# Transposing the activations on VectorE in 32x32 blocks, with both batches interleaved, in a two-layer graph network

## The chip, the cores and the metric

The kernel runs on one core of one Trainium2 chip. A core has TensorE (matmuls and transposes through the array, results in PSUM), VectorE, ScalarE and GpSimd (elementwise work), and a sync engine that only issues DMA transfers here. SBUF is the on-chip memory of 128 partitions, PSUM the matmul output[...]. The metric is the device time of one execution in microseconds (us). The profiles call the engines PE, DVE, ACT and POOL; PEld is TensorE's weight load, SPq the sync engine's queue.

## The reference

64 batches of 256 tokens with 512 features, all in fp32, go through two layers, each with a layer norm, a ReLU and a residual. The first multiplies by an adjacency matrix over the tokens and then by a weight; the second is masked attention with 8 heads.

```python
# x: (64, 256, 512)   adj: (256, 256)   all weights: (512, 512)
h = jnp.maximum(_layernorm(x, axis=-1), 0.0)
x = x + jnp.einsum('bnd,do->bno', jnp.einsum('nm,bmd->bnd', adj, h), L0_weight) + L0_bias
h = jnp.maximum(_layernorm(x, axis=-1), 0.0)
q, k, v = (h @ W + b split into 8 heads of 64, for Wq, Wk, Wv)
scores = jnp.einsum('bqhd,bkhd->bhqk', q, k) / 8 + (1.0 - adj) * -1e9
out = jnp.einsum('bhqk,bkhd->bqhd', softmax(scores), v)
x = x + out.reshape(b, n, d) @ Wo + bo
```

## The kernel before

The batches are taken in 32 groups of two (`GB = 2`, `NT = 2` tiles of 128 tokens per batch, `T = 4` tiles per group, `DC = 4` chunks of 128 features). The five projections (w, q, k, v, o) each use seven products of half-size blocks in place of eight (a Strassen-like form); one product is 4 matmuls of 256 columns, and an fp32 matmul shows up as two instructions in the trace.

A program in Python lays out every engine's instructions in one fixed order. `after(delay, fn)` puts work off by so many ticks, and a `yield` of a projection is one tick. PSUM banks are handed out in the order in which they were given back:

```python
    def bank(shape, name):
        i = free_banks.pop(0)
        ...
    def give(t):
        free_banks.append(bank_of.pop(id(t))[0])
```

The features must lie on the partitions for q, k and v, so the normalised activations h1 are transposed by TensorE and copied from PSUM to `h1T`; then GpSimd forms the differences t1 to t4 for the seven products:

```python
    def queries_keys(g):
        ...
        h1T = act.tile([P, DC, GN], F32, tag="bT", name=f"h1T_{g}")
        halves = H1T[g] = Halves(f"h_{g}", [h1T[:, d, :] for d in range(DC)])
        for t in range(T):
            ps = bank([P, DC, P], f"ph_{g}_{t}")
            for d in range(DC):
                nc.tensor.transpose(ps[:, d, :], h1[:, t, d * P:(d + 1) * P], ident)
            if t % 2:
                nc.vector.tensor_copy(h1T[:, :, t * P:(t + 1) * P], ps)
            else:
                nc.scalar.copy(h1T[:, :, t * P:(t + 1) * P], ps)
            give(ps)
        for c in range(2):
            halves.sums(nc.gpsimd, c, ("t1", "t2"))
        for c in range(2):
            halves.sums(nc.gpsimd, c, ("t3", "t4"))
        yield
```

A projection. `read` and `finish` take a bank's partial result out, in the output projection by VectorE (`x <- o_a, x`); the product with `s2` adds to bank `pa` after `read(pa, 1)`:

```python
    def project(s, halves, by_token, name, read, finish, first_half_first=False):
        pa = new("a")
        product(pa, s, "a11", halves, "b11", by_token, stop=False)     # 1st product
        u1 = read(pa, 1)
        yield
        ...
        pb = new("b")
        product(pb, s, "a12", halves, "b21", by_token)                 # 2nd
        finish(pb, u1, 0, 0)
        give(pb)
        yield
        product(pa, s, "s2", halves, "t2", by_token, start=False, stop=False)   # 3rd
        u2 = read(pa, 2)
        yield
        ...  # 4th: s1 t1 into pc; 5th: s3 t3 into pa; 6th: a22 t4 into pd; 7th: s4 b22 into pc
```

`b11` to `b22` are blocks of the transposed activations themselves, t1 to t4 their differences. In q and k the activations are the moving operand of the matmul, in v the stationary one (the weight load).

The scores of a group and half of the heads: four rounds (c, b) of matmuls into two banks, two evictions by VectorE and a subtraction by GpSimd each:

```python
    def score(g, qd):
        for c in range(2):
            for b in range(GB):
                ps = [bank([P, NT * N], f"sc_{g}_{qd}_{c}{b}_{j}") for j in range(2)]
                ... # matmuls
                for j in range(2):
                    nc.vector.scalar_tensor_tensor(a[...], ps[j], SCALE, maskT_f, op0=ALU.mult, op1=ALU.add)
                    give(ps[j])
                nc.gpsimd.tensor_tensor(a, a, top_b, op=ALU.subtract)
                after(3 + 2 * c + b, exponent, a)
                after(5 + 2 * c + b, key_sum, g, qd, c, b)
```

The steady loop. `attend` is the attention product pav with the softmax denominator pden, `post` the output projection of the group before, `layer0` the first layer of the group after the next:

```python
    for g in range(NG):
        attend(g, 0)
        score(g, 1)
        tick()
        if g > 0:
            run(post(g - 1))
        if g + 2 < NG:
            load(g + 2)
            ready(g + 2, 6)
        if g + 1 < NG:
            run(queries_keys(g + 1))
        ...
        attend(g, 1)
        if g + 1 < NG:
            score(g + 1, 0)
        tick()
        if g + 1 < NG:
            run(values(g + 1))
        if g + 2 < NG:
            run(layer0(g + 2))
```

Of the kernel before, what the change touches and what calls it, by code (L numbers as in the profile page):

```python
# [8 lines left out]
F32 = mybir.dt.float32  # L9
I32 = mybir.dt.int32  # L10
AF = mybir.ActivationFunctionType
ALU = mybir.AluOpType
AX = mybir.AxisListType
P = 128
# [184 lines left out]
def kernel(  # L199
# [56 lines left out]

    clock, later = [0], []

    def after(delay, fn, *args):
        later.append((clock[0] + delay, len(later), fn, args))  # L260

    def tick():
        clock[0] += 1
        due = sorted(e[:2] for e in later if e[0] <= clock[0])
        run_now = [e for d in due for e in later if e[:2] == d]
        later[:] = [e for e in later if e[0] > clock[0]]
        for _, _, fn, args in run_now:
            fn(*args)

    X, H0, Q, K, V, OT, HO = {}, {}, {}, {}, {}, {}, {}  # L270

    def load(g):
        X[g] = xpool.tile([P, T, D], F32, tag="x", name=f"x_{g}")
        src = x[g * GB:(g + 1) * GB].rearrange("b (t p) d -> p (b t) d", p=P)
        for t in range(0, T, 1 if g == 0 else T):
            e = t + (1 if g == 0 else T)
            nc.sync.dma_start(X[g][:, t:e, :], src[:, t:e, :])

# [3 lines left out]


    load(0)
    adj_sb = tmp.tile([P, NT, N], F32, tag="u", name="adj_sb")
    nc.sync.dma_start(adj_sb, adj.rearrange("(t p) m -> p t m", p=P))
# [26 lines left out]

    adjT = const.tile([P, NT, N], F32, name="adjT")
    pa = bank([P, NT, N], "pa")
    for k in range(NT):
        for t in range(NT):
            nc.tensor.transpose(pa[:, k, t * P:(t + 1) * P], adj_sb[:, t, k * P:(k + 1) * P], ident)
    nc.vector.tensor_copy(adjT, pa)
# [7 lines left out]
    def masks():  # L327
        nc.vector.tensor_scalar(maskT, adjT, -1.0, 1.0, op0=ALU.mult, op1=ALU.add)
        nc.vector.tensor_scalar(maskT, maskT, MASKED, None, op0=ALU.mult)
        nc.vector.tensor_scalar(adj_sb, adj_sb, -1.0, 1.0, op0=ALU.mult, op1=ALU.add)  # L330
        nc.vector.tensor_scalar(adj_sb, adj_sb, MASKED, None, op0=ALU.mult)
        rowmax = small.tile([P, NT], F32, tag="rowmax", name="rowmax", bufs=1)
        nc.vector.tensor_reduce(rowmax, adj_sb, AX.X, ALU.max)
        spread = tmp.tile([P, NT, P], F32, tag="u", name="spread")
        nc.vector.tensor_copy(spread, rowmax[:, :, None].to_broadcast([P, NT, P]))
        pt = bank([P, N], "pt")
        for t in range(NT):
            nc.tensor.transpose(pt[:, t * P:(t + 1) * P], spread[:, t, :], ident)
        nc.vector.tensor_copy(top, pt)
        give(pt)  # L340
# [16 lines left out]


    def weight_sums(eng, w, name):
        def part(i, j):  # L360
            return w[:, 2 * j:2 * j + 2, i * HF:(i + 1) * HF]
        s = {n: const.tile([P, 2, HF], F32, name=f"{name}_{n}") for n in ("s1", "s2", "s4")}
        eng.tensor_tensor(s["s1"], part(1, 0), part(1, 1), op=ALU.add)
        eng.tensor_tensor(s["s2"], s["s1"], part(0, 0), op=ALU.subtract)
        eng.tensor_tensor(part(1, 0), part(0, 0), part(1, 0), op=ALU.subtract)
        eng.tensor_tensor(s["s4"], part(0, 1), s["s2"], op=ALU.subtract)
        s.update(a11=part(0, 0), a12=part(0, 1), a22=part(1, 1), s3=part(1, 0))
        return s

    class Halves:  # L370

        def __init__(self, name, chunks):
            self.chunks = chunks
            self.t = {n: act.tile([P, 2, N], F32, tag="t", name=f"{n}_{name}", bufs=8)
                      for n in ("t1", "t2", "t3", "t4")}

        def b(self, j, k, c):
            return self.chunks[2 * j + c][:, k * N:(k + 1) * N]

# [9 lines left out]
    def product(ps, s, a, halves, b, by_token, start=True, stop=True):  # L389
        for m in range(2):  # L390
            for c in range(2):
                w, y = s[a][:, c, :], halves.operand(b, c)
                lhs, rhs = (y, w) if by_token else (w, y)
                nc.tensor.matmul(ps[:, m, :], lhs[:, m * P:(m + 1) * P], rhs, start=(start and m + c == 0), stop=(c == 1),  # L394
                                 skip_group_check=True)
# [71 lines left out]

    H1, H1T = {}, {}

    def layer0(g):  # L470
# [3 lines left out]
        yT = act.tile([P, DC, GN], F32, tag="bT", name=f"yT_{g}")  # L474
        halves = Halves(f"y_{g}", [yT[:, d, :] for d in range(DC)])
        for d in (0, 2, 1, 3):
# [15 lines left out]
        st = [small.tile([P, 2, nc.vector.BN_STATS_DIM], F32, tag="st1", name=f"st1_{g}_{t}", bufs=8) for t in range(T)]  # L492
        h1 = H1[g] = act.tile([P, T, D], F32, tag="h", name=f"h1_{g}")
        done = []
# [19 lines left out]

        yield from project(W0, halves, True, f"w_{g}", read, finish)

    def queries_keys(g):

        xt, h1 = X[g], H1.pop(g)
        h1T = act.tile([P, DC, GN], F32, tag="bT", name=f"h1T_{g}")  # L520
        halves = H1T[g] = Halves(f"h_{g}", [h1T[:, d, :] for d in range(DC)])
        for t in range(T):
            ps = bank([P, DC, P], f"ph_{g}_{t}")
            for d in range(DC):
                nc.tensor.transpose(ps[:, d, :], h1[:, t, d * P:(d + 1) * P], ident)  # L525
            if t % 2:
                nc.vector.tensor_copy(h1T[:, :, t * P:(t + 1) * P], ps)  # L527
            else:
                nc.scalar.copy(h1T[:, :, t * P:(t + 1) * P], ps)
            give(ps)  # L530
        for c in range(2):
            halves.sums(nc.gpsimd, c, ("t1", "t2"))
        for c in range(2):
            halves.sums(nc.gpsimd, c, ("t3", "t4"))
        yield

        def out_bias_add(t):
            nc.gpsimd.tensor_tensor(xt[:, t, :], xt[:, t, :], bo_r, op=ALU.add)  # L538

        for s, bias, store, n in ((WQ, bq_c, Q, "q"), (WK, bk_c, K, "k")):  # L540
            store[g] = {}
# [14 lines left out]
            if n == "k":  # L556
                for t in range(T):
                    after(2 * t + 1, out_bias_add, t)
            yield from project(s, halves, False, f"{n}_{g}", read, finish)

    def values(g):
# [13 lines left out]

        yield from project(WV, halves, True, f"v_{g}", read, finish)

    def post(g):

        xt = X.pop(g)  # L580
        halves = HO.pop(g)
        done = []

        def read(ps, n):
            o = quarter(xt, *RESIDUAL[n])
            add(o, ps, o)

        def finish(ps, u, i, k):
            o = quarter(xt, i, k)
            add(o, ps, o)  # L590
            done.append(k)
            if done.count(k) == 2:
                nc.sync.dma_start(out[g * GB + k].rearrange("(t p) d -> p t d", p=P), xt[:, k * NT:(k + 1) * NT, :])

        yield from project(WO, halves, True, f"o_{g}", read, finish, first_half_first=g == NG - 1)

    A, AS = {}, {}

    def score(g, qd):


        for c in range(2):
            for b in range(GB):
# [8 lines left out]
                for j in range(2):  # L612
                    nc.vector.scalar_tensor_tensor(a[:, j * NT:(j + 1) * NT, :].rearrange("p k n -> p (k n)"),  # L613
                                                   ps[j], SCALE, maskT_f, op0=ALU.mult, op1=ALU.add)
                    give(ps[j])
                nc.gpsimd.tensor_tensor(a, a, top_b, op=ALU.subtract)  # L616
                after(3 + 2 * c + b, exponent, a)
                after(5 + 2 * c + b, key_sum, g, qd, c, b)

# [3 lines left out]
    def key_sum(g, qd, c, b):  # L623
        s = AS[c, b] = att.tile([P, 2, N], F32, tag=f"as{c}{b}", name=f"as_{g}_{qd}_{c}{b}")
        a4 = A[c, b].rearrange("p (j k) n -> p j k n", j=2)
        nc.gpsimd.tensor_tensor(s, a4[:, :, 0, :], a4[:, :, 1, :], op=ALU.add)  # L626

    def attend(g, qd):
# [21 lines left out]
        chunks = OT.setdefault(g, [])  # L650
        chunks += o
        nc.scalar.activation(den, pd, AF.Identity, accum_out=stats[:, 0, i:i + 1])  # L652
# [4 lines left out]

        def divide():
            for f in range(2):
                nc.vector.tensor_tensor(o[f], po[f], rden, op=ALU.mult)  # L660
                give(po[f])
            nc.scalar.activation(den, rden, AF.Identity, accum_out=stats[:, 1, i:i + 1])
            if qd == (0 if g == NG - 1 else 1):
                HO[g] = Halves(f"o_{g}", chunks)
                for c in range(2):
                    HO[g].sums(nc.gpsimd, c, ("t1",))
            if qd == 1:
                for which in ("t2",), ("t3", "t4"):
                    for c in range(2):
                        HO[g].sums(nc.gpsimd, c, which)  # L670

# [11 lines left out]
    for _ in range(T + 1):  # L683
        tick()
    W0 = weight_sums(nc.gpsimd, w0_sb, "w0")
    for _ in range(T + 2):
# [4 lines left out]
    run(first, 3)  # L691
    WQ = weight_sums(nc.gpsimd, wq_sb, "wq")
    run(first)
    first = queries_keys(0)
    run(first, 1)
    WK = weight_sums(nc.gpsimd, wk_sb, "wk")
    run(first, 5)
    WV = weight_sums(nc.gpsimd, wv_sb, "wv")
    out_bias()
    ready(1, 0)  # L700
    run(first)
    WO = weight_sums(nc.gpsimd, wo_sb, "wo")
    score(0, 0)
    run(values(0))
    run(layer0(1))
    for g in range(NG):
        attend(g, 0)
        score(g, 1)
        tick()
# [65 lines left out]
```

## Time and profile before

The time is 2839.26 us, the median of three runs (2838.41 to 2841.76). The profiled execution spans 2840.6 us at a granted TensorE clock of 0.997.

| group of instructions | count | busy us | mean ns of one |
|---|---|---|---|
| POOL score subtraction (L616), 128x1024 | 256 | 597.1 | 2368 |
| DVE score eviction (L613), 128x512 | 512 | 311.9 | 681 |
| DVE reciprocal (L656), 128x128 | 256 | 231.8 | 926 |
| PE first-layer product py (L480), 256 columns | 1024 | 229.3 | 382 |
| PE transposes ph (L525), 128x128 | 512 | 63.0 | 276 |
| PEld of those transposes | 512 | 58.7 | 143 |
| DVE copy h1T<-ph (L527), 128x512 | 64 | 44.0 | 690 |
| ACT copy h1T<-ph (L529), 128x512 | 64 | 37.4 | 585 |
| POOL difference t_h<-h1T (L387), 128x256 | 128 | 92.8 | 725 |

Busy time is the time in which at least one instruction of the group ran; the mean of one is longer than busy time over count where instructions overlap, as TensorE's do. From start to start, a steady product of eight matmul instructions takes 1.73 us, and the 16 transposes of a group 1.98 us. Transfers: a load of x (1 MB) lands 5.4 us after its issue, an output of 512 KB 2.8 us after, a `bv_c` transfer of 0.2 KB 2.0 us after.

Two things help in reading what follows. In a timeline a row's end is its start plus its duration, but TensorE's modelled ends overlap the next start, so for TensorE starts are compared with starts. And a share of busy time says which engine is full, not which wait ends last in a given stage.

### The profile page before, as it was taken

What the parts mean: (1) busy time and instruction counts of PE and PEld (TensorE: products, weight loads), DVE (VectorE), ACT (ScalarE), POOL (GpSimd) and SP (SyncE); (2) the same over time, 40 slices, a digit from 0 to 9 for tenths busy, and PEclk for the clock granted to TensorE, in tenths of its full rate; (3) what the DMA queues carried; (4) which work ended last, traced back from release to release, by engine and by line L of the source; (5) the groups of instructions that cost most, each with busy time, mean ns of one, the idle gap of its engine ahead of it and who ended that gap; (6) DMA issues with size and microseconds to landing.
All of it is one profiled execution on the core that took longest, in us unless ns stands there. A gap on an engine that the chain in (4) does not pass through costs nothing.

```text
span 2840.6 us, 43306 instructions
## 1 busy us (share of the span) xinstructions
PE 2799.5 (99%) x17680; PEld 2301.5 (81%) x17680; DVE 1478.2 (52%) x2703; ACT 851.7 (30%) x1441; POOL 1882.6 (66%) x1754
## 2 busy tenths in 40 slices
PE   6999999999999999999999999999999999999998
PEld 5788888888888888888888888888888888888886
DVE  3454545545555445455455554455554555545545
ACT  2332323323223233233232332332322323323221
POOL 5766666767567676676665676756766656767565
PEclk9999999999999999999999999999999999999999
DMA  4000000000000000000000000000000000000000
GB/s 130 1 1 30 31 31 30 1 30 31 31 31 21 11 30 31 30 31 1 30 31 31 30 16 16 30 31 31 30 1 30 31 31 31 10 22 30 31 16 31
DMA packets 39563, 75.97 MB, mean 27 GB/s; under 512 B 3520, under 2 KB 3776, under 8 KB 39360
## 3 DMA queue, kind: packets, MB, share of 16 engines
q1 hardware_dynamic: 39360, 73.15, 7.5%
q8 instruction: 141, 2.31, 0.3%
q14 instruction: 62, 0.51, 0.1%
HBM read 39.59 MB, written 33.55 MB: 26 GB/s over the span
## 4 chain that ended last, share of the span: by engine, by line
PE 96%; POOL 2%; DVE 1%; issue 1%; DMA 0%; ACT 0%; SPq 0%; DVEq 0%; POOLq 0%; ACTq 0%
PE sc L608 8%; PE py L480 8%; PE pav L638 8%; PE pden L644 2%; PE ph L525 2%; POOL a L616 1%; DVE x L441 0%; DVE a L613 0%; DMA adj_sb<-in_adj_dram 0%; PE q_0a L394 0%; PE o_25a L394 0%; PE o_17a L394 0%; PE o_5a L394 0%; PE o_7a L394 0%; PE o_4a L394 0%
## 5 line engine op out<-in xcount | busy, mean ns | idle before, releaser
L616 POOL TENSOR_TENSOR a<-a,top 128x1024 f32<-128x1024 f32 x256 | 597.1, 2368 | 189.0 <-DVE a L613 189.0
L53 POOL TENSOR_TENSOR rs<-rs,mhalf 128x2 f32<-128x2 f32 (+1 forms) x96 | 77.6, 809 | 553.9 <-DVE nb L52 553.9
L613 DVE SCALAR_TENSOR_TENSOR a<-sc,maskT 128x512 f32<-128x512 f32 x512 | 311.9, 681 | 230.1 <-PE sc L608 230.1
L626 POOL TENSOR_TENSOR as<-a 128x512 f32<-128x512 f32 x256 | 317.9, 1282 | 0.3 <-ACT a L621 0.3
L621 ACT ACTIVATE a<-a 128x1024 f32<-128x1024 f32 x256 | 266.7, 1054 | 136.6 <-POOL a L616 136.6
L608 PE MATMUL sc<-q,k 64*128 64x256 f32 x2048 | 250.1, 384 | 0.0
L608 PEld LDWEIGHTS sc<-q,k 64*128 64x128 f32 x2048 | 205.3, 186 | 45.5 <-PE pden L644 25.5
L480 PE MATMUL py<-adjT,h 128*128 128x256 f32 x1024 | 229.3, 382 | 6.7 <-ACT h L458 6.7
L512 ACT ACTIVATE h<-x,nb,rs 128x512 f32<-128x512 f32 x128 | 97.2, 806 | 460.6 <-POOL nb L54 460.6
L638 PE MATMUL pav<-a,v 128*32 128x256 f32 x4096 | 234.3, 381 | 0.0
L656 DVE RECIPROCAL rden<-den 128x128 f32<-128x128 f32 x256 | 231.8, 926 | 4.6 <-ACT den L652 4.6
L460 POOL TENSOR_TENSOR x<-x,b_r 128x512 f32<-128x512 f32 x128 | 162.5, 1282 | 103.2 <-ACT h L458 103.2
L480 PEld LDWEIGHTS py<-adjT,h 128*128 128x128 f32 x1024 | 196.4, 192 | 34.3 <-ACT h L458 7.4
L638 PEld LDWEIGHTS pav<-a,v 128*32 128x32 f32 x4096 | 126.5, 110 | 98.2 <-issue 21.2
L538 POOL TENSOR_TENSOR x<-x,bo_r 128x512 f32<-128x512 f32 x128 | 162.5, 1271 | 0.0
L482 ACT COPY yT<-py 128x512 f32<-128x512 f32 x128 | 75.0, 586 | 223.8 <-PE py L480 223.8
L387 POOL TENSOR_TENSOR t_h<-h1T 128x256 f32<-128x256 f32 x128 | 92.8, 725 | 72.8 <-DVE h1T L527 72.8
L458 ACT ACTIVATE h<-x,nb,rs 128x512 f32<-128x512 f32 x128 | 96.4, 806 | 11.0 <-POOL nb L54 11.0
L504 DVE BATCH_NORM_STATS2 st<-x 128x6 f32<-128x256 f32 x256 | 96.4, 419 | 4.4
L387 POOL TENSOR_TENSOR t_o<-oT,t_o 128x256 f32<-128x256 f32 x128 | 93.3, 743 | 7.8 <-DVE oT L660 7.8
L387 POOL TENSOR_TENSOR t_y<-yT,t_y 128x256 f32<-128x256 f32 x128 | 92.9, 726 | 5.8 <-ACT yT L482 0.8
L387 POOL TENSOR_TENSOR t_h<-h1T,t_h 128x256 f32<-128x256 f32 x128 | 92.8, 725 | 5.0
(2950 smaller groups left out, 5550.1 us busy)
## 6 DMA issues: line engine op xcount, KB each, us to landing
out_dram<-x SPq DMA_DIRECT2D x64, 512.0 KB, 2.8
x<-in_x_dram SPq DMA_DIRECT2D x31, 1024.0 KB, 5.4
x<-in_x_dram SPq DMA_DIRECT2D x4, 256.0 KB, 3.7
w_sb<-in_L_gnn_weight_dram SPq DMA_DIRECT2D x1, 1024.0 KB, 8.3
wq_sb<-in_L_gnn_Wq_dram SPq DMA_DIRECT2D x1, 1024.0 KB, 11.2
wk_sb<-in_L_gnn_Wk_dram SPq DMA_DIRECT2D x1, 1024.0 KB, 12.2
wv_sb<-in_L_gnn_Wv_dram SPq DMA_DIRECT2D x1, 1024.0 KB, 12.2
wo_sb<-in_L_gnn_Wo_dram SPq DMA_DIRECT2D x8, 128.0 KB, 4.6
```

The lines of the kernel that those rows point to most:

```text
L387: eng.tensor_tensor(self.t[n][:, c, :], self.operand(p, c), self.operand(q, c), op=ALU.subtract)
L460: nc.gpsimd.tensor_tensor(xt[:, t, :], xt[:, t, :], b0_r, op=ALU.add)
L480: nc.tensor.matmul(ps[:, b * N:(b + 1) * N], h[:, b * NT + k, d * P:(d + 1) * P], adjT[:, k, :], start=(k == 0), stop=(k == NT - 1))
L512: nc.scalar.activation(h1[:, k * NT + t, :], xt[:, k * NT + t, :], AF.Relu, bias=nb[:, t:t + 1], scale=rs[:, t:t + 1])
L538: nc.gpsimd.tensor_tensor(xt[:, t, :], xt[:, t, :], bo_r, op=ALU.add)
L608: nc.tensor.matmul(ps[j][:, kt * N:(kt + 1) * N], k[j * HD:(j + 1) * HD, c, kt * P:(kt + 1) * P], q[j * HD:(j + 1) * HD, c, :], start=True ...
L613: nc.vector.scalar_tensor_tensor(a[:, j * NT:(j + 1) * NT, :].rearrange("p k n -> p (k n)"), ps[j], SCALE, maskT_f, op0=ALU.mult, op1=ALU.add)
L616: nc.gpsimd.tensor_tensor(a, a, top_b, op=ALU.subtract)
L621: nc.scalar.activation(a, a, AF.Exp)
L626: nc.gpsimd.tensor_tensor(s, a4[:, :, 0, :], a4[:, :, 1, :], op=ALU.add)
L638: nc.tensor.matmul(po[f][h * 32:(h + 1) * 32, b * N:(b + 1) * N], v[:, k, h * HD + f * 32:h * HD + f * 32 + 32], A[h // 2, b][:, (h % 2) * ...
L656: nc.vector.reciprocal(rden[:, c * P:(c + 1) * P], den[:, c * P:(c + 1) * P])
```

## The change

TensorE's transposes of h1 are taken away from group 2 on. VectorE transposes h1 instead: one instruction transposes each 32x32 block of a 128x512 tile within its own block position, and writes the two batches alternately, so that an element of batch 0 is followed by that of batch 1. What remains, the move of blocks between partitions, is done by 16 transfers from SBUF to SBUF per group (one for each pair of a source and a target strip of 32 partitions) in runs of 512 bytes: 2 token tiles x 32 tokens x 2 batches x 4 bytes. So that those runs are contiguous, the tokens of a tile are permuted by blocks of 32: x is loaded and out is stored in eight transfers of 32 partitions per group, adjT is built from a permuted adjacency, and the division writes its output in permuted order (four instructions of 256 in place of two of 512). The purpose is to free TensorE of the transposes and the two engines of the copies that followed them.

With it go: h1T is read with a step of two elements; the tiles t1 to t4 have 4 buffers in place of 8, which makes room for the new tile `r`; the differences for the output projection (`out_sums`) are formed at the head of the next round in place of after the division; the key sums of the second half come four ticks later; the mask is transposed separately from adjT. Groups 0 and 1 keep TensorE's transposes, with copies that interleave.

The core of the diff (cuts marked with ...; left out are the bookkeeping of `after` and `tick`, the renaming of the weight tables and the forms of `Halves` and `product` for a stepped block):

```diff
@@ load
-        src = x[g * GB:(g + 1) * GB].rearrange("b (t p) d -> p (b t) d", p=P)
-        for t in range(0, T, 1 if g == 0 else T):
-            e = t + (1 if g == 0 else T)
-            nc.sync.dma_start(X[g][:, t:e, :], src[:, t:e, :])
+        src = x[g * GB:(g + 1) * GB]
+        for k in range(GB):
+            for i in range(NI):
+                nc.sync.dma_start(X[g][32 * i:32 * i + 32, k * NT:(k + 1) * NT, :], by_block(src, i)[:, k])
@@ adjacency
+    for i in range(NI):
+        nc.sync.dma_start(adj_r[32 * i:32 * i + 32], by_block(adj[None], i)[:, 0])
...
+    for u in range(NT):
+        nc.vector.tensor_copy(adj_p[:, u, :].rearrange("p (t i b) -> p i t b", i=NI, t=NT),
+                              adj_r[:, u, :].rearrange("p (i t b) -> p i t b", i=NI, t=NT))
...
     def masks():
-        nc.vector.tensor_scalar(maskT, adjT, -1.0, 1.0, op0=ALU.mult, op1=ALU.add)
+        pm = bank([P, NT, N], "pm")
+        for k in range(NT):
+            for t in range(NT):
+                nc.tensor.transpose(pm[:, k, t * P:(t + 1) * P], adj_sb[:, t, k * P:(k + 1) * P], ident)
+        nc.vector.tensor_scalar(maskT, pm, -1.0, 1.0, op0=ALU.mult, op1=ALU.add)
@@ Halves
-            self.t = {n: act.tile([P, 2, N], F32, tag="t", name=f"{n}_{name}", bufs=8)
+            self.t = {n: act.tile([P, 2, N], F32, tag="t", name=f"{n}_{name}", bufs=4)
@@ end of layer0
+        h1T = act.tile([P, DC, N, GB], F32, tag="bT", name=f"h1T_{g}")
+        H1T[g] = [h1T[:, d].rearrange("p n k -> p k n") for d in range(DC)]
+        if g < 2:
+            ...   # TensorE's transposes as before, copies of 128x128 that interleave
+            return
+        r = act.tile([P, DC * NI, NT, 32, GB], F32, tag="r", name=f"r_{g}")
+        def turn(k):
+            for t in range(NT):
+                nc.vector.transpose(r[:, :, t, :, k], h1[:, k * NT + t, :].rearrange("p (j b) -> p j b", b=32))
+        def turn_last():
+            turn(1)
+            blocks = r.rearrange("p (d j) t b k -> p j d (t b k)", j=NI)
+            for i in range(NI):
+                for j in range(NI):
+                    nc.sync.dma_start(h1T[32 * j:32 * j + 32, :, 64 * i:64 * i + 64, :].rearrange("p d n k -> p d (n k)"),
+                                      blocks[32 * i:32 * i + 32, j])
+        turn(0)
+        TURN[g] = turn_last
@@ queries_keys
-        ...   # the four transposes and copies shown above
@@ score: between() is turn_last of the next group
                 nc.gpsimd.tensor_tensor(a, a, top_b, op=ALU.subtract)
+                if between and c + b == 0:
+                    between()
                 after(3 + 2 * c + b, exponent, a)
-                after(5 + 2 * c + b, key_sum, g, qd, c, b)
+                after((5 if qd == 0 else 9) + 2 * c + b, key_sum, g, qd, c, b)
@@ attend, divide
             for f in range(2):
-                nc.vector.tensor_tensor(o[f], po[f], rden, op=ALU.mult)
+                for k in range(GB):
+                    ...   # dst and src of 256, dst in the permuted order
+                    nc.vector.tensor_tensor(dst, src, den_k, op=ALU.mult)
                 give(po[f])
...
-            if qd == 1:   # the differences of the output projection
-                ...
+            if g == NG - 1:
+                out_sums(g, ("t1",) if qd == 0 else ("t2", "t3", "t4"))
@@ post
-                nc.sync.dma_start(out[g * GB + k].rearrange("(t p) d -> p t d", p=P), xt[:, k * NT:(k + 1) * NT, :])
+                for i in range(NI):
+                    nc.sync.dma_start(by_block(out[g * GB:(g + 1) * GB], i)[:, k],
+                                      xt[32 * i:32 * i + 32, k * NT:(k + 1) * NT, :])
@@ the loop
         attend(g, 0)
-        score(g, 1)
+        if g > 0:
+            out_sums(g - 1)
+        score(g, 1, TURN.get(g + 1) if g > 0 else None)
```

## The prediction

> **What bounds the kernel now.** I read the page from the top: busy shares, then the chain that ended last, then one group of two batches in the order of time.
>
> ```profile
> PE 2799.5 (99%) x17680; PEld 2301.5 (81%) x17680; DVE 1478.2 (52%) x2703; ACT 851.7 (30%) x1441; POOL 1882.6 (66%) x1754
> ...
> PE 96%; POOL 2%; DVE 1%; issue 1%; DMA 0%; ACT 0%; SPq 0%; DVEq 0%; POOLq 0%; ACTq 0%
> ```
>
> TensorE is busy 99% of the span and 96% of the closing chain; the other engines are far from full. So a microsecond off TensorE's list is a microsecond off the total, unless TensorE then waits. Whether it waits is not seen in shares, so I take the timeline of group 16, TensorE and then VectorE (start, duration, engine, line, operation):
>
> ```profile
> 1417.92 3.66 PE L638 MATMUL pav<-a,v 128*32 128x256 f32 x64
> ...
> 1422.37 4.09 PE L608 MATMUL sc<-q,k 64*128 64x256 f32 x32
> 1426.39 1.99 PE L394 MATMUL o_14a<-wo_sb,oT 128*128 128x256 f32 x8
> 1428.22 1.89 PE L394 MATMUL o_14b<-wo_sb,oT 128*128 128x256 f32 x8
> 1429.95 1.98 PE L394 MATMUL o_14a<-wo_s,t_o 128*128 128x256 f32 x8
> ...
> 1438.73 1.91 PE L525 MATMUL ph<-ident,h 128*128 128x128 f32 x16
> 1440.71 1.97 PE L394 MATMUL q_16a<-h1T,wq_sb 128*128 128x256 f32 x8
> ```
>
> ```profile
> 1421.15 0.16 DVE L52 TENSOR_SCALAR nb<-mv 128x2 f32<-128x2 f32 x1
> 1423.61 4.87 DVE L613 SCALAR_TENSOR_TENSOR a<-sc,maskT 128x512 f32<-128x512 f32 x8 [2.29 <-PE sc L608]
> 1428.40 0.94 DVE L656 RECIPROCAL rden<-den 128x128 f32<-128x128 f32 x1
> 1429.26 0.62 DVE L441 TENSOR_TENSOR x<-o_14a,x 128x512 f32<-128x512 f32 x1
> ```
>
> Put the zero at 1417.92, where the attention product pav begins. TensorE runs without a break: pav and den to 4.45, scores to 8.47, seven products of the output projection of 1.73 each from start to start, the transposes (ph) from 20.81 to 22.79, then q. The transposes hold TensorE for 1.98 us per group; one period (w_16a at 1405.64 to w_17a at 1492.67) is 87.03 us.
>
> The second fence shows what the first hides. The third output product adds to the bank of the first, which VectorE must have read (x<-o_14a). That read ends at 1429.26 + 0.62 = 1429.88, and the third product starts at 1429.95: 0.07 us later. VectorE is only half busy overall, yet **from the first score eviction (5.69) to this read (11.96) it has no gap and sets TensorE's pace to within 0.07 us**. Anything put into that stretch of VectorE is paid by TensorE.
>
> [...] The interleaved h1T has a step of two fp32, 8 bytes[...]. TensorE reads no stepped operand in the rows I rest on, so no run here shows it. [...]the contiguous subtraction takes 725 ns here. [...] The trace has no such instruction; its 512-element instructions have a start-to-start step of (4.87 - 0.68)/7 = 0.60 us, which I take for a transpose of 512 elements. [...]0.2 KB lands in 2.0 us, 512 KB in 2.8.
>
> **The change part by part**, groups 2 to 31 (30 of them; 0 and 1 keep TensorE's transposes).
>
> Removed: 16 transposes, 1.98 us of TensorE; two h1T copies on VectorE (690 ns) and two on ScalarE (585 ns), all behind the seventh product.
>
> Added on VectorE: four transposes. The first two (batch 0) stand behind the last norm scale, which ends at 1421.15 + 0.16 = 3.39, and wait for the first two h rows (two at 806 ns from 2.52, ends 4.04). Ends about 5.3, before the scores want VectorE at 5.69: free. The other two stand between the first and second pair of score evictions. Their input (ScalarE's second h pair) is there at 5.93, and the first pair ends near 7.0, so they wait for nothing, but push the six later evictions, the reciprocal and x<-o_a back by 2 x 0.60 = 1.2 us. The read that ended at 11.96 ends at 13.2, the third product starts at about 13.25 in place of 12.03: **1.2 us of new wait on TensorE**. The first product is late on the way too (its bank is that of the third eviction: about 0.5), but that lies inside the 1.2. Later reads have slack: the fifth product waits for a read that ended 0.8 before it started. The division as four instructions of 256 in place of two of 512 adds some 0.3, behind this point.
>
> From the third product to the end of the projection is 1438.73 - 1429.95 = 8.78. So q can start at 13.25 + 8.78 = 22.03, where it starts at 22.79 now: **0.76 us saved per group** of the 1.98.
>
> The transport: the 16 transfers are issued from about 8.3, when the last transpose is done. At the start of the trace small transfers are issued every 0.47 us:
>
> ```profile
> 25.06 0.42 SPq L302 DMA_DIRECT2D wo_sb<-in_L_gnn_Wo_dram  x1
> 25.53 0.42 SPq L303 DMA_DIRECT2D bv_c<-in_L_gnn_bv_dram  x1
> 26.00 0.43 SPq L302 DMA_DIRECT2D wo_sb<-in_L_gnn_Wo_dram  x1
> ```
>
> 16 x 0.47 = 7.5; with 2.0 to 2.8 to land they are there at about 18.3, against 22.0 when q asks: 3.7 us in hand.
>
> GpSimd: the output projection's differences (8 x 0.69 = 5.5) move in front of the score subtractions (9.34), because the four t tiles are now shared. It is free at about 4.4, so 4.4 + 5.5 + 9.3 = 19.2; then h's t1 and t2 (4 x 0.69) are done at 22.0, and q's third product wants them at 22.0 + 3.5. Free, with 3.5 us in hand.
>
> Start: adjT needs four transfers of 32 rows, two VectorE copies and then the transposes (about +1). The mask is made from its own TensorE transposes, which stand behind the first py product, and its VectorE chain (0.68 + 0.43 + 0.42 + 0.43 + 0.69 + 0.68 = 3.3) must end before the pt transposes that stand ahead of the second py product. Now that chain runs before py and hides. Mask transposes about 0.8, chain 3.3, and the 1: +5 us once. The stepped copies of groups 0 and 1 and the four output transfers at the end: +1. At the end GpSimd sums the keys before the output differences, which may take away the two waits of 1.15 and 0.59 on pden: -1.
>
> Sum: 2839.3 - 30 x 0.76 (22.8) + 5 = **2821 us**.
>
> **The rivals.** *The wait does not come* (the transposes find a gap, or finish sooner): all 1.98 stays, 59 us, and the total is 2839 - 59 + 5 = 2785. Against it: the 0.07 us above. For it: the pacing chain is seen at the resolution of one group. *Slower transposes*: at double, 1.2 us each, the wait is 2.4 and the first pair also pushes the scores by about 0.8; a group then loses 1.2, and the total is about 2880. Nothing in the trace tells against a half rate for fp32. *The transport is late*: each microsecond beyond the 3.7 in hand costs 30 us. A transfer waits for the one eight before it, so landing in over 8 x 0.47 = 3.8 us would slow the issue as well; 512-byte runs are not in the trace at this place. *The stepped operand*: three of the seven products of q, of k and of v read h1T itself. If a stepped moving operand ran at half speed, q and k would lose 6 x 1.73 = 10.4 us per group, 311 in all, and the total would pass 3100; for v the stepped side is the weight load, which has room (190 of about 379 ns).
>
> **Range and chances.** The main estimate moves with the transpose: 0.55 to 0.75 us each gives a wait of 1.1 to 1.5, a saving of 0.9 to 0.5 per group, and 2818 to 2830. The start is good to 2 us. The range 2788 to 2852 takes in nearly all of the no-wait rival and a late transport by one microsecond. Faster by over 2% needs less than 2782.5, which even the no-wait rival just misses: 0.12. Slower by over 2% needs 2896: a stepped-operand loss, a late transport by over 2 us, or slow transposes together with something else: 0.09.
>
> **What would show it.** In the changed profile: TensorE busy about 2740 (480 transposes of 0.123 us gone); the period near 86.3; idle time of some 1.2 us per group ahead of the third output product (or split with the first), released by VectorE's x<-o read; transposes of 600 to 700 ns on VectorE; issues of h1T every 0.47 us, and no idle time of q's first product that ends with a transfer; q's and k's matmuls still 379 ns; t_h still 725 ns; w_0a some 5 us later than 26.82. If q's first product waits for a transfer, the transport was mis-sized; if TensorE is busier than before, the stepped read is not free; if the third product starts without a wait, my chain through VectorE was wrong.

## The result and the profile after

The changed kernel takes **2832.9 us** (median of 4 runs, 2831.99 to 2835.19) against 2840.12 us for the kernel before (4 runs, the earlier ones among them): ratio 0.9976, 95% interval 0.9959 to 0.9993. The change gains 7.2 us where 18 had been forecast. The two lines of the page that answer to those shown before, busy shares and closing chain:

```profile
PE 2757.9 (97%) x17204; PEld 2254.2 (80%) x17204; DVE 1531.5 (54%) x2905; ACT 821.0 (29%) x1393; POOL 1886.7 (67%) x1754
...
PE 90%; DVE 8%; issue 1%; POOL 0%; SPq 0%; DMA 0%; ACT 0%; DVEq 0%; POOLq 0%; ACTq 0%
```

TensorE has lost 476 instructions and 41.6 us, but its share fell to 97%, and VectorE, 1% of the closing chain before, holds 8% of it. TensorE now waits for VectorE. Where, the timeline of group 16 shows, TensorE first:

```profile
1413.93 3.66 PE L699 MATMUL pav<-a,v 128*32 128x256 f32 x64
...
1422.74 1.99 PE L416 MATMUL o_14a<-wo_sb,oT 128*128 128x256 f32 x8 [0.27 <-DVE a L665]
1424.58 1.89 PE L416 MATMUL o_14b<-wo_sb,oT 128*128 128x256 f32 x8
1427.23 1.97 PE L416 MATMUL o_14a<-wo_s,t_o 128*128 128x256 f32 x8 [0.77 <-DVE x L463]
...
1435.99 1.98 PE L416 MATMUL q_16a<-h1T,wq_sb 128*128 128x256 f32 x8
1437.80 1.97 PE L416 MATMUL q_16b<-h1T,wq_sb 128*128 128x256 f32 x8
1439.61 1.89 PE L416 MATMUL q_16a<-t_h,wq_s 128*128 128x256 f32 x8
```

and VectorE beside it:

```profile
1419.62 1.29 DVE L665 SCALAR_TENSOR_TENSOR a<-sc,maskT 128x512 f32<-128x512 f32 x2 [0.90 <-PE sc L660]
1420.82 1.29 DVE L563 STREAM_TRANSPOSE r<-h 128x512 f32<-128x512 f32 x2
1422.04 3.64 DVE L665 SCALAR_TENSOR_TENSOR a<-sc,maskT 128x512 f32<-128x512 f32 x6
1425.61 0.93 DVE L717 RECIPROCAL rden<-den 128x128 f32<-128x128 f32 x1
1426.46 0.62 DVE L463 TENSOR_TENSOR x<-o_14a,x 128x512 f32<-128x512 f32 x1
```

Put the zero again where pav begins, 1413.93. The pair of transposes stands between the second and the third eviction without a gap, the read of the first product ends at 13.15, the third product starts at 13.30 and q at 22.06. The waits of 0.27 and 0.77 us in brackets are the new ones, and they are all that TensorE waits for in this period of 86.70 us: it is busy for 85.66 of it.

One thing more is new, and no wait shows it. From the start of q_16b to that of the third product of q it is 1.81 us (1437.80 to 1439.61). Before it was 1.73:

```profile
1442.51 1.89 PE L394 MATMUL q_16b<-h1T,wq_sb 128*128 128x256 f32 x8
1444.24 1.91 PE L394 MATMUL q_16a<-t_h,wq_s 128*128 128x256 f32 x8
```

The trace says how long one matmul takes; the rows are those of q_16b, minimum, median and maximum in ns, first of the kernel before, then of the changed one:

```profile
L394 PE MATMUL q_16b<-h1T,wq_sb x8: 379/379/379, 1442.5 to 1444.0; 128*128 128x256 f32 x8
```

```profile
L416 PE MATMUL q_16b<-h1T,wq_sb x8: 385/388/388, 1437.8 to 1439.4; 128*128 128x256 f32 x8
```

The stage of q and k (from q_16a to the pav behind it) takes 25.17 us (1435.99 to 1461.16) where it took 24.75 (1440.71 to 1465.46). Five of the six products that read h1T itself are 0.08 to 0.09 us longer, which makes the 0.42; the sixth, q_16a, took 1.80 already before, right behind the transposes, and takes 1.81.

For everything that follows I take the period over the whole steady part, (start of v_31a - start of v_1a)/30 from each profile: **87.05 us before, 86.68 after**.

### The profile page after: what moved, and what is told of

Read it like the earlier page. It is cut to its first block, busy times and chain, and to the rows that moved or that the text cites. A ratio compares the mean times of both kernels' runs of the same rounds, so it can differ in the third digit from the quotient of the medians.

```text
span 2831.6 us, 44124 instructions
## 1 busy us (share of the span) xinstructions
PE 2757.9 (97%) x17204; PEld 2254.2 (80%) x17204; DVE 1531.5 (54%) x2905; ACT 821.0 (29%) x1393; POOL 1886.7 (67%) x1754
## 4 chain that ended last, share of the span: by engine, by line
PE 90%; DVE 8%; issue 1%; POOL 0%; SPq 0%; DMA 0%; ACT 0%; DVEq 0%; POOLq 0%; ACTq 0%
PE pav L699 8%; PE py L502 8%; PE sc L660 5%; DVE a L665 4%; PE pden L705 2%; DVE r L563 1%; DVE rden L717 1%; DVE x L463 1%; PE q_0a L416 0%; PE v_22a L416 0%; PE v_21a L416 0%; PE v_19a L416 0%; PE v_17a L416 0%; PE v_16a L416 0%; PE v_14a L416 0%
## 5 line engine op out<-in xcount | busy, mean ns | idle before, releaser
L660 PEld LDWEIGHTS sc<-q,k 64*128 64x128 f32 x2048 | 205.4, 186 | 45.1 <-PE pden L705 13.2
L409 POOL TENSOR_TENSOR t_y<-yT 128x256 f32<-128x256 f32 x128 | 93.5, 731 | 30.6 <-ACT yT L504 30.6
```

The lines of the kernel that those rows point to most:

```text
L409: eng.tensor_tensor(self.t[n][:, c, :], self.operand(p, c), self.operand(q, c), op=ALU.subtract)
L660: nc.tensor.matmul(ps[j][:, kt * N:(kt + 1) * N], k[j * HD:(j + 1) * HD, c, kt * P:(kt + 1) * P], q[j * HD:(j + 1) * HD, c, :], start=True ...
```

## The experiments

Two theories, which the expectations call S and V. **S**: the moving operand with a step of 8 bytes costs each product that reads h1T itself some 0.08 us, and this ate the missing part. **V**: the rest is VectorE's chain from the evictions to the first reads; whatever is put into it, TensorE waits for. Their rivals: the transposed layout has nothing to do with the matmuls' length (other traffic, the transfers), or the transport or GpSimd holds q up.

| kernel | median us | ratio to before (95%) | period us |
|---|---|---|---|
| changed kernel | 2832.9 | 0.9976 (0.9959 to 0.9993) | 86.68 |
| e1_before_stepped | 2855.2 | 1.0054 (1.0040 to 1.0068) | 87.53 |
| e2_apart | 2818.7 | 0.9921 (0.9908 to 0.9935) | 86.16 |
| e3_invert_late | 2816.0 | 0.9914 (0.9901 to 0.9928) | 85.95 |
| e4_turn_twice | 2867.6 | 1.0096 (1.0080 to 1.0111) | 87.87 |
| e5_mask_early | 2827.8 | 0.9949 (0.9936 to 0.9963) | 86.68 |
| e6_apart_late | 2799.5 | 0.9857 (0.9842 to 0.9872) | 85.48 |
| e7_best | 2800.1 | 0.9861 (0.9846 to 0.9876) | 85.55 |
| e9_mask_apart_late | 2791.5 | 0.9826 (0.9813 to 0.9839) | 85.53 |
| e10_turn_after_evictions | 2789.3 | 0.9819 (0.9805 to 0.9832) | 85.39 |

**e1_before_stepped**: the kernel before with nothing but the interleaved h1T.

```diff
-        h1T = act.tile([P, DC, GN], F32, ...)
+        h1T = act.tile([P, DC, N, GB], F32, ...)
-                nc.vector.tensor_copy(h1T[:, :, t * P:(t + 1) * P], ps)
+                nc.vector.tensor_copy(h1T[:, :, (t % NT) * P:(t % NT + 1) * P, t // NT], ps)
```

> The kernel before with one edit: h1T is stored with the two batches interleaved, so that q and k read a moving operand with a step of two elements; TensorE's transposes stay, nothing is carried by transfers. Theory S (a stepped moving operand costs TensorE about 0.08 us per product): q's and k's products on h1T go from 1.73 to 1.81 us from start to start, v's stay at 1.73, a period grows by about 0.42 us and the total by 13 us, to about 2853 (ratio 1.0047). Rival R (the longer products in the changed kernel come from the transfers or from the other order of work beside them, not from the step): products stay at 1.73 and the total at 2840.

```profile
L394 PE MATMUL q_16b<-h1T,wq_sb x8: 387/388/388, 1445.9 to 1447.4; 128*128 128x256 f32 x8
```

The 388 ns are here without VectorE's transposes, without transfers and without permuted tokens. The period grows by 0.48 us, the total by 15 us; in group 16 no wait is added (q_21a alone waits, 0.4 us for a copy). S holds for the step alone.

**e2_apart**: the changed kernel, the batches kept apart in `r` and h1T, so that the transfers run in 256 bytes instead of 512.

```diff
-        h1T = act.tile([P, DC, N, GB], F32, ...)
+        h1T = act.tile([P, DC, GB, N], F32, ...)
-        r = act.tile([P, DC * NI, NT, 32, GB], F32, ...)
+        r = act.tile([P, NI, DC, GB, NT, 32], F32, ...)
```

> The changed kernel with the batches apart again: VectorE writes the transposes batch by batch and the 16 transfers write runs of 256 bytes in place of 512, twice as many. Theory S: all of q's and k's products take 1.73 us, and where the transport is still in time the period falls from 86.68 to 86.27 and the total by about 12 us to 2821. If an issue grows with the number of runs (0.66 us now for 128 runs, up to 1.3 for 256), the 16 take up to 21 us, h1T lands some 10 us too late and the total rises by up to 300 us. Rival R: products stay at 1.81.

```profile
L416 PE MATMUL q_16b<-h1T,wq_sb x8: 379/379/380, 1432.5 to 1434.1; 128*128 128x256 f32 x8
```

The 379 ns are back, the period falls by 0.52 us and the total by 14 us, while the waits on VectorE stay (0.28 and 0.76). Twice as many runs of half the length did not hold the transport up: the 16 issues took 11.36 us against 10.76, and q waited for none of them. Together with e1 this closes the missing part from both sides.

**e3_invert_late**: the changed kernel, the reciprocals and the division one tick later, so that the first reciprocal stands behind x<-o_a instead of ahead of it.

```diff
-            after(1 + c, invert, c)
-        after(5, divide)
+            after(2 + c, invert, c)
+        after(6, divide)
```

> The changed kernel with the four reciprocals and the division one tick later, so that VectorE reads the first output product before the first reciprocal (0.87 us) and not after it. Theory V (the wait of the third output product is VectorE's chain of evictions, transposes, reciprocal and read): the wait of 0.77 us goes, the 0.27 ahead of the first product stays, the period falls by 0.75 to about 85.9 and the total by 23 us to about 2810 (ratio 0.989). Rival: another wait of about the same length (GpSimd's t_o, or h1T's landing, which comes 1.1 us before q asks) takes its place and the total stays near 2833.

```profile
1414.74 1.99 PE L416 MATMUL o_14a<-wo_sb,oT 128*128 128x256 f32 x8 [0.27 <-DVE a L665]
...
1418.42 1.97 PE L416 MATMUL o_14a<-wo_s,t_o 128*128 128x256 f32 x8
```

The 0.77 us ahead of the third product are gone, the period is 0.73 us shorter, and the total falls by 17 us. That is less than the 23 expected: 30 x 0.73 are 22, but in the profiles v_1a comes 2.7 us later and the end takes 0.4 us more; what is left of the difference is within the spread of the runs. Moving the reciprocals and the division by one tick, which made nothing cheaper, was worth more than the whole change.

**e4_turn_twice**: the second pair of transposes done twice.

```diff
             turn(1)
+            turn(1)
```

> The changed kernel with the second pair of transposes done twice, in the same place (the second time over the first, the result is the same). Theory V: each extra pair is paid in full, about 1.2 us per group, 30 x 1.2 = 37 us, total about 2870; the h1T transfers are issued 1.2 us later as well and q, which starts 1.2 us later, still finds them. Rival (VectorE's chain has slack of its own, and the waits seen come from elsewhere): much less than 37 us.

```profile
1443.71 1.99 PE L416 MATMUL o_14a<-wo_sb,oT 128*128 128x256 f32 x8 [1.45 <-DVE a L666]
...
1448.20 1.97 PE L416 MATMUL o_14a<-wo_s,t_o 128*128 128x256 f32 x8 [0.76 <-DVE x L463]
```

Two more transposes, 2 x 0.60 us, and TensorE pays 1.18 more ahead of the first product; the period grows by 1.19. V holds to within 0.02 us. Note the place: the first product's bank comes from the third eviction, so work ahead of that eviction is paid there, and the third product's wait stays as it was.

**e5_mask_early**: the mask moved ahead of the first layer-0 group.

```diff
+    masks()
     first = layer0(0)
-    run(first, 1)
-    masks()
-    run(first, 3)
+    run(first, 4)
```

> The changed kernel, with the whole of masks() (its four transposes and its VectorE chain) moved ahead of the first layer-0 group, so that the chain no longer stands between the first adjacency products and the transposition of them; nothing else is moved. Prediction as on record: the changed start costs 4.3 us that the end keeps, so taking it away should give about 4 us back (about 2829 us against 2833, ratio to the kernel before about 0.996). Rival, from the trace of the changed kernel: the first groups are held by GpSimd's sums, which absorbed most of the delay (v_0a is 6.1 us later than before, q_1c only 0.8 us later), so the total moves by under 1.5 us, and the first adjacency products earn a lead that is gone by v_1a.

The period is unchanged to 0.01 us and the total falls by 5.1 us (the runs of the two kernels don't overlap): the rival, which was my own reading of one pair of profiles, falls. In that pair v_1a was only 1.2 us later after the change than before it, and I took the delay for absorbed. Over all profiles but those of the runs with a step on adjT (last below), v_1a is at 164.4 and 167.9 with the start of the kernel before, at 169.1 to 172.0 in the six with the changed start (mean 170.5), at 162.8, 165.5 and 166.7 in the three with the early mask. These are one profile of each kernel, so the kernels differ a little too; but the five runs of this one kernel also lie 6.2 us apart (2823.6 to 2829.8). The scatter is as large as what I had read from a single pair. The means say 4.3 us lost by the changed start, 5.5 regained by the early mask, both uncertain by some microseconds.

Why the chain was dear: VectorE's rows in the changed kernel, then the same operations before (where the mask is made ahead of the first py product):

```profile
21.17 1.00 DVE L349 TENSOR_SCALAR maskT<-maskT 128x512 f32<-128x512 f32 x1
22.09 1.48 DVE L350 TENSOR_SCALAR adj_sb<-adj_sb 128x512 f32<-128x512 f32 x1
23.61 1.37 DVE L351 TENSOR_SCALAR adj_sb<-adj_sb 128x512 f32<-128x512 f32 x1
```

```profile
14.60 0.43 DVE L329 TENSOR_SCALAR maskT<-maskT 128x512 f32<-128x512 f32 x1
14.94 0.42 DVE L330 TENSOR_SCALAR adj_sb<-adj_sb 128x512 f32<-128x512 f32 x1
```

In the changed kernel GpSimd worked without a gap from 15.60 on (weight sums and bias sums of 1.27 us); before, this run of sums began at 15.83, behind VectorE's rows. The lengths of these rows go with that: 0.42 us ahead of the sums (GpSimd was then on an operation of 128x4), 1.00 to 1.48 beside them. The early mask of e5_mask_early splits the same chain over both cases, as GpSimd's sums begin at 16.00 there:

```profile
15.57 0.42 DVE L350 TENSOR_SCALAR adj_sb<-adj_sb 128x512 f32<-128x512 f32 x1
16.02 1.52 DVE L351 TENSOR_SCALAR adj_sb<-adj_sb 128x512 f32<-128x512 f32 x1
```

The row ahead of the sums takes 0.42 us (1.48 in the changed kernel), the one beside them 1.52. So three profiles show that the length goes with GpSimd's sums; what in the hardware makes it so was not shown.

**e6_apart_late**: e2 and e3 together.

> The changed kernel with both repairs that the earlier runs named: the batches kept apart in the transposed activations (q, k products with an unstepped moving operand) and the reciprocals and the division one tick later (no wait ahead of the third output product). If the two gains are independent, the period is 86.15 - 0.7 = about 85.4 us and the total about 2818.7 - 17 = 2800 us (ratio 0.986). Rival: the transport is the next wait. In the changed kernel GpSimd got the transposed activations 20.98 us after the zero and q started at 22.06; in this kernel q would start at about 21.2, and the four sums behind the arrival need some 0.6 us each, so part of the gain comes back as waits of the q products on GpSimd or on the transfers: then period about 85.8 and total about 2809 us.

Period 85.48 us, total 2799.5. The two gains add up: 0.52 + 0.73 = 1.25 of expected fall, 1.20 measured. In group 16 GpSimd began on h1T 21.22 us after the start of pav and q began at 21.26, so the transport now has nothing in hand; in five other groups q waits 0.3 to 0.7 us, in the longest case (q_12a) for the transfers by name.

**e7_best**: e6 with the second pair of transposes behind the first read, and two issuing queues.

```diff
-                    nc.sync.dma_start(h1T[32 * j: ...
+                    (nc.scalar if j % 2 else nc.sync).dma_start(h1T[32 * j: ...
-        score(g, 1, TURN.get(g + 1) if g > 0 else None)
+        score(g, 1)
...
+            p = post(g - 1)
+            next(p)
+            TURN[g + 1]()   # where the next group has one
+            tick()
+            run(p)
```

> The kernel of e6_apart_late with two more edits: the second pair of transposes is issued after the first output product has been read rather than ahead of the score evictions' end, and the 16 transfers are shared by two issuing queues (SyncE's and ScalarE's). Theory V: the 0.28 us ahead of the first output product goes too, and the transfers' later start (about 1 us) is more than made up by two queues (issue 16 x 0.66 = 10.6 us becomes 5.3 us), so period about 85.1 and total about 2791 us (ratio 0.983). Rival: ScalarE, which now issues eight transfers in its own order, holds up the score evictions or exponentials behind them by up to 8 x 0.6 = 4.8 us a group, and TensorE waits on it: then period above 86.

The period is 85.55 us, no better than e6. Neither theory had it. The 0.28 us ahead of the first product are gone, as V said. The rival was right in its first half: behind its eight issues ScalarE starts the first exponential 18.43 us after the start of pav in place of 12.21, more than the 4.8 us allowed for; but TensorE waits for none of that. The chain that ended last shows what took the place of the 0.28 us ("issue" is time for which the profile names no releaser):

```profile
1418.65 1.79 PE o_14c L416 x8
1420.44 0.40 issue
1420.84 1.97 PE q_16a L416 x8
```

The transfers, issued from 12.4 us after the start of pav in place of 8.3, are 0.4 us late for q. This is read from the times: the last issue begins at 1417.4, a transfer lands up to 3.2 us later, GpSimd too begins on h1T only at 1420.80, and in e6 and e9, which issue the same 16 transfers, waits of q are put down to the transfers by name (0.7 us in one group; 0.5, 0.6 and 0.9 us in three). Two queues cut the issuing from 10.94 to 6.01 us, where 5.3 had been expected, and a transfer took 3.0 us to land in place of 2.2.

**e9_mask_apart_late** and **e10_turn_after_evictions**: e6 with the early mask; and the same with the transposes between the last eviction and the first read, and two queues.

> The kernel of e6_apart_late with masks() ahead of the first layer-0 group, as in e5_mask_early. If the start and the steady part are independent, the start's gain (v_1a came 3.6 us earlier in e5_mask_early than in the changed kernel) adds to the period's: 2799.5 - 4 = about 2795 us, ratio about 0.984, period still 85.4 to 85.5. Rival: the early start is eaten by a wait in groups 0 to 2, and the total stays at 2799.

> The kernel of e9_mask_apart_late with the second pair of transposes between the last score eviction and the read of the first output product, and the 16 transfers shared by SyncE's and ScalarE's queues. In e7_best the pair stood after that read, the first output product waited for nothing, and q waited 0.40 us for the transfers; here they begin about 0.7 us earlier, which is more than that, while the read is 1.2 us later. Expected: no wait ahead of the first output product, at most 0.25 us ahead of the third (its bank is read at about 1.9 + 1.2 us after the evictions), none ahead of q: period about 85.2 to 85.3, total about 2788 us. Rival: the third product waits the whole 0.8 us again (period 85.9, total 2806), or q still waits 0.4 us (total as e9_mask_apart_late).

e9 came to 2791.5 us; the start's gain and the period's add up and even somewhat more (8 us less than e6, the period within 0.05 us). e10 came to 2789.3 us, period 85.39. In it neither the first product nor q waits, and the third product has this left:

```profile
1402.30 1.99 PE L416 MATMUL o_14a<-wo_sb,oT 128*128 128x256 f32 x8
1404.13 1.89 PE L416 MATMUL o_14b<-wo_sb,oT 128*128 128x256 f32 x8
1406.32 1.97 PE L416 MATMUL o_14a<-wo_s,t_o 128*128 128x256 f32 x8 [0.30 <-DVE x L463]
```

The two intervals overlap, so which is faster is not settled. Both are 1.7 to 1.8% faster than the kernel before, that is some 50 us, seven times what the change brought as it stood.

**e8_step16, e11_step12, e12_step8**: the kernel before with a step on another moving operand, adjT in the py products.

```diff
-    adjT = const.tile([P, NT, N], F32, name="adjT")
+    adjT4 = const.tile([P, N, 4], F32, name="adjT")       # 3 for 12 bytes, 2 for 8 bytes
+    adjT = adjT4[:, :, 0:NT].rearrange("p n k -> p k n")
-            self.t = {n: act.tile([P, 2, N], F32, tag="t", ..., bufs=8)
+            self.t = {n: act.tile([P, 2, N], F32, tag="t", ..., bufs=7)
```

> The kernel before, with the transposed adjacency (the moving operand of the 16 py products of a group) stored with a step of 16 bytes instead of 4, and nothing else in its place changed but one buffer fewer for the weight-sum operands to make room. The step of 8 bytes cost a product of eight matmuls 0.08 to 0.09 us (1.73 to 1.81), that is 0.0105 us a matmul on a spacing of 0.216 us. If the cost grows with the bytes that are passed over, py's 16 matmuls go from 0.216 to about 0.25 us each or more (0.5 us and up a group); if it is a fixed toll on any step other than one element, to about 0.227 (0.17 us a group, as for 8 bytes); if four bytes out of every 16 or more halve the reading, to about 0.43 (3.4 us a group).

> As e8_step16, with a step of 12 bytes instead of 16. With 16 bytes the 1,024 py matmuls took 629 ns instead of 382 each by the profile and the total grew by 283 us, that is 0.28 us a matmul on a spacing of 0.216; with 8 bytes the q and k matmuls took 0.0105 us more. If what counts is whether two elements lie in the same 16 bytes, a step of 12 bytes (where one element in four of them shares its 16 bytes with the next, and three elements fall in 48 bytes) lies between: some 0.15 to 0.25 us more a matmul, total 2990 to 3100 us. If only multiples of 16 bytes are dear (all elements in the same place of their 16 bytes), it costs as little as 8 bytes: about 11 us in all, 2851 us.

> As e8_step16 and e11_step12, with a step of 8 bytes on the same operand, which closes the row: the 32 py matmuls of a group took 0.216 us each from start to start with a step of 4 bytes, 0.340 with 12 and 0.450 with 16, that is 1.57 and 2.08 times as long. The 16-byte pieces that 256 elements touch are 64, 192 and 256; 128 with 8 bytes. If the time is set by the pieces touched, two elements to a piece being the full rate, with a fixed toll of 4 to 5% on any step, then 12 and 16 bytes should be 1.5 and 2.0 times the 8-byte time, which makes it 0.226 us a matmul (7.23 us a group in place of 6.91, total about 2851 us). If the 1.05 of the stepped q and k products was theirs alone, py stays at 0.216 and the total at 2841.

One group's 32 py matmuls in the timeline of, in this order, the kernel before, and the steps of 8, 12 and 16 bytes:

```profile
1398.73 7.07 PE L480 MATMUL py<-adjT,h 128*128 128x256 f32 x32
```

```profile
1421.71 7.41 PE L481 MATMUL py<-adjT,h 128*128 128x256 f32 x32
```

```profile
1475.48 11.04 PE L481 MATMUL py<-adjT,h 128*128 128x256 f32 x32
```

```profile
1441.18 14.60 PE L481 MATMUL py<-adjT,h 128*128 128x256 f32 x32
```

From their start to that of the product behind them it is 6.91, 7.25, 10.87 and 14.41 us. The expectation of e12 is met to 0.02 us (7.23). Of the three ways named for 16 bytes, halving came closest (0.43 us a matmul, 0.450 measured), though its "3.4 us a group" counts 16 of the 32 instructions. With 12 bytes a matmul costs 0.124 us more and not 0.15 to 0.25; that the total of 3007 fell into the range named is luck, for it holds something else. The totals (2893, 3007 and 3123 us) are no measure of the step: in all three a w product also waits some 1.2 us for GpSimd's t_y in 30 of the 32 groups, which the kernel before doesn't do. The buffer that was taken away for the room is the likely cause; that was not tried by itself.

## Why the prediction was right or wrong

1. **The bound and the wait: right.** The read was to end at 13.2 and the third product to start at 13.25: 13.15 and 13.30. q was to start at 22.03: 22.06. Of the 0.76 us per group 0.73 were there when q began (22.79 less 22.06), and e3 and e4 show that the chain through VectorE is the cause, in both directions.

2. **The transpose: right.** 0.60 us was assumed; two took 1.22 us from start to start (1420.82 to 1422.04) and pushed the third eviction by that much, and e4's two more cost 1.18.

3. **The stepped operand: the step that failed.** The working took a step of 8 bytes as free, which was the author's estimate and stood in no row of the trace, and put "q's and k's matmuls still 379 ns" into the sum. They take 388, and a product 1.81 us in place of 1.73. That makes 0.42 us a group (stage of q and k; 0.52 by e2, where q_16a too is down to 1.72); the prediction's period of "near 86.3" (87.03 - 0.76 = 86.27) becomes 86.27 + 0.42 = 86.69, and 86.68 was measured. (With the 0.73 of point 1 it is 86.72; the rest is in the w products, 12.23 us from w_16a to pav in place of 12.28.) Over 30 groups that is 12.6 us, more than the gap of 10.8 between the gains forecast and measured. The rival named the right place with the wrong size: it weighed half speed (10.4 us a group) against nothing, and a toll of 5% on a small share of the products was not in the list. One of the signs named could not have shown it either: "TensorE is busier than before" fails although the step is not free, for the 480 transposes of 0.123 us that went (59 us) outweigh a toll of 13 to 17. For v, whose stepped side is the weight load, the reasoning held: 1.73 us a product before and after.

4. **The transport: right that it hides, mis-sized.** 16 issues were put at 7.5 us and landing at 18.3, with 3.7 in hand. The queue of the sync engine, then GpSimd's first use of the result:

```profile
1422.25 10.76 SPq L570 DMA_DIRECT2D h1T<-r  x16
```

```profile
1434.91 0.61 POOL L409 TENSOR_TENSOR t_h<-h1T 128x256 f32<-128x256 f32 x1 [1.82 <-DMA h1T<-r]
```

An issue of these takes about 0.67 us on average (0.60 in the median, up to 1.10) and not 0.47, the last landing lets GpSimd start at 20.98, and GpSimd, which was free at 19.16 (predicted 19.2), waits 1.82 us for it. Only 1.1 us were in hand ahead of q, which cost nothing here and limits what e6 and e7 could gain. The 0.47 came from loads from DRAM at the start, a different kind of transfer. The other fear, that a transfer waits for the one eight before it, can be seen in the trace of the kernel before: the 18th and the 20th transfer, both to bv_c, are issued at 18.33 and 23.76, when the 10th (wk_sb, 6.07 + 12.2) and the 12th (wv_sb, 11.56 + 12.2) have landed, after waits of 1.5 and 4.6 us. It did not bite here: a transfer to h1T lands 2.1 us after its issue (median; at most 3.2 in group 16 and 3.9 in the whole run), before eight issues of 0.60 us have passed.

5. **GpSimd's stepped read: right.** A difference that reads h1T takes 731 ns on average against 725.

6. **Start and end: about right.** +5 was put down for the start. That the sum came near is partly luck: the mask chain takes 5.8 us from its first row to the end of `spread` in place of the 3.3 worked out, w_0a came at 33.4 and not 5 but 6.6 us later than 26.8, and some of that was absorbed on the way; the mean over profiles is 4.3 us at v_1a. The end was to come out even (+1 and -1); from v_31a to the end it is 62.2 us against 61.3, so +0.9: the waits on pden are gone, the smaller output transfers at the end take more.

7. **TensorE busy about 2740: missed at 2758**, for the reason in 3: 0.42 to 0.52 us for 32 groups are 13 to 17 of the 18 us.

With the measured terms the sum is -30 x (87.05 - 86.68) + 4.3 + 0.9 = -5.9 us, against -7.2 measured with an interval of about -11.6 to -2.0.

## What to carry to other kernels

Before a layout with a step is adopted because it makes a transfer's runs longer, price the step on the engine that is the bound: here 4 to 5% on its operand (1.73 to 1.81 us a product) outweighed the transfers, which were hidden either way in runs of 512 and of 256 bytes (10.76 and 11.36 us of issuing). When work is moved off the bound engine, look at where on its new engine it lands; moving a neighbour that nobody needs yet, here the reciprocals, can be worth more than the move itself. And one pair of profiles doesn't show what a start costs, where profiles with the same start lie three microseconds apart.

## What the runs showed of the hardware

From a step of 8 bytes on, the time of the fp32 moving operand grew in proportion to the step: with steps of 4, 8, 12 and 16 bytes, 32 matmuls of 256 columns took 6.91, 7.25, 10.87 and 14.41 us. From 8 bytes on that is 1 : 1.50 : 1.99, while the unstepped read is not twice as fast as 8 bytes but only 4.9% faster. The pieces of 16 bytes that e12's expectation counts (64, 128, 192 and 256) stand in the same ratios from 8 bytes on; a step of more than 16 bytes, where the two readings part, was not run, so which of them sets the time was not shown. A step of 8 bytes itself cost 4 to 5% (a py matmul 0.216 to 0.227 us, q and k products 1.73 to 1.81 us). As the stationary operand of v the same tensor cost nothing: its weight load rose from 190 to 196 ns beside a matmul of 379.

The 64 KB transfers from SBUF to SBUF took 0.67 us of the sync engine each with 128 runs of 512 bytes and 0.71 with 256 of 256 bytes (10.76 and 11.36 us for 16), where the first loads from DRAM took 0.47. Two queues at once brought 16 of them to 6.0 us in e7, at 3.0 us to land in place of 2.2 in e6.
